# A new order of work for the last twenty steps of a recommendation kernel on Trainium2

## The chip, the cores and the metric

The kernel runs on one core of one Trainium2 chip. The core has a matmul engine (TensorE, PE in the profile, with its weight loads shown as PEld), three engines for elementwise work (VectorE or DVE, ScalarE or ACT, GpSimd or POOL) and SyncE (SP), which only issues DMAs. Each engine works through its own instructions in the order in which the program gives them, and they meet through semaphores. The metric is device time in microseconds; the median of several runs is compared.

## What is computed

The reference embeds a batch of 16384 users with 69 feature ids each, and one label id per user, from a table of 100001 rows of 96 floats. A small attention net weighs each feature's row against the label's row; the weighted rows are summed by 10 groups of features; a top net of three layers gives one number per user. In short:

```python
u  = emb[batch_user]                       # [B, 69, 96]
ql = emb[batch_label[:, 0]]                # [B, 96]
z  = concat([q, u, q - u, q * u])          # q: ql beside each feature
h  = dice(z @ W1 + b1, a1)                 # 64 wide
att = (h @ W2 + b2) @ W3 + b3              # one weight per feature
pre = where(batch_user < ITEM_NUM, u * att, 0)
pooled = einsum('gf,bfe->bge', window, pre)
x  = concat([pooled, ql])                  # 11 x 96
h  = dice(bn(x @ Wf1 + bf1), af1)          # 200 wide
h  = dice(bn(h @ Wf2 + bf2), af2)          # 80 wide
y  = h @ Wf3 + bf3
```

`dice(x)` is `(alpha * (1 - p) + p) * x` with `p` a sigmoid of the scaled `x`. All is float32.

## The kernel before

**Tiles.** The batch is cut into 32 blocks of 512 users (`BLK`). Of the 69 features 64 are "main" and 5 are "tail". A chunk is 512 rows of the table, four gathers of 128: a main chunk holds 8 users with their 64 features, a tail chunk holds one feature of all 512 users. A block has 64 + 5 = 69 chunks, and two chunks make a pair, so that there are 1104 pairs (`NPAIR`). The program is a list of steps, one per pair, and one more at the end. In the last block the tail chunks are put after the first 20 main ones (`chunk_of`).

**What a step holds.** `fetch(i)` (line 359) gathers the eight tiles of pair `i` by GpSimd's indirect DMA (line 266), transposes each on TensorE into a bank of PSUM (`ptr`), and lets VectorE copy the bank out twice: as it is (`uT`, line 376) and multiplied by the label's row (`quT`, line 379). For some chunks one of the four tiles comes instead by 128 row DMAs, each of one row, issued by SP or ACT (line 301) into a ring of buffers; `scalar_rows(i)` issues 20 of ACT's in each of the first 1088 steps.

`hidden(i)` (line 389) is called the sums in the change's description: four matmuls into one bank (`ph`, lines 396 to 403), two activations on ScalarE (lines 405, 406) and a product on VectorE (line 407) give `y`. `attend_tail` (line 419) turns `y` into weighted tail features. `attend_rows(b, n)` (line 409) takes `n` pairs from `b` on, a band: it forms rows of attention weights on TensorE (`prow`) and copies them on ScalarE (`row`). `spread(b, n)` (line 427) transposes a band (`patt`) and lets VectorE form the pooling weights `rw` (line 436). `pool(i)` (line 448) multiplies the gathered tiles with these weights into the bank `acc`, of which there is one, and VectorE copies the sums into `pooled` (line 470).

**The top net.** `top_steps(n, cols)` (line 542) cuts it into ten works: four parts of the first layer for each half of its 200 outputs (`top1`, line 489, with `dice` on ScalarE and VectorE after the fourth), the second layer (`top2`) and the third (`top3`, or `top3_last` for the last users). The last block's users are taken in four quarters of 128 columns, and `quarter[r]` is the list of ten works of quarter `r`.

**The order of work.** No scheduler moves anything: `plan` maps a step to a list of works, `at(step, ...)` appends to it, and the loop at the end (line 681) calls them in that order. The order of the works is therefore the order on each engine's queue. With `c = NPAIR - CLOSE = 1096`, the steps before `c - 8` follow one pattern: rows of bands of four, tails three steps behind the gathers, sums two behind, poolings seven behind (`POOL_LAG`). From `c - 8` on the poolings, and from `c` on everything, are written out step by step; in steps `c + 3` to `c + 7` some works are called between the two chunks of a `fetch`.

**Buffers.** Gathered pairs live in 15 buffers (`upool`). PSUM has eight banks: two for transpositions (`ps_tr`), two for the sums (`ps_h`), two for rows, spreads and tails (`ps_x`), one for the poolings (`ps_acc`) and one for the top net (`ps_m`). The second half of the first layer takes a bank of `ps_h` instead of `ps_m` in the last two quarters.

Of the kernel before, what the change touches and what calls it, by code (L numbers as in the profile page):

```python
# [18 lines left out]
P = 128  # L19
B, F, E, G = 16384, 69, 96, 10  # L20
# [5 lines left out]
BLK = 512  # L26
NBLK = B // BLK
# [5 lines left out]
NQ = BLK // P  # L33
NT = NCH * 4
NCOL = NT + NQ
NPAIR = NBLK * NCH // 2
# [4 lines left out]
POOL_LAG = 7  # L41
# [3 lines left out]
EARLY = 20  # L45

CLOSE = 8


ROW_BYTES = 4 * E  # L50
# [65 lines left out]
def rec_kernel(  # L116
# [372 lines left out]
    def top1(n, cols, h, part, p1):  # L489

        if part == 0:

            banks, tag = (ps_h, "h") if n == NBLK - 1 and cols.start >= BLK // 2 and h == 1 else (ps_m, "m")
            p1 = banks.tile([DH, BLK], F32, tag=tag, name=f"p1_{n}_{h}_{cols.start}")[:, cols]
        for k in range(part * KTOP // 4, (part + 1) * KTOP // 4):
            if k < NTAIL:
                w, x = V[:, k], pres[n][:, k, cols]
            elif k == NTAIL:
                w, x = wf1[:, G], qTs[n % 2][0:E, cols]
            else:  # L500
                w, x = wf1[:, k - NTAIL - 1], pooled[n][:, k - NTAIL - 1, cols]
            nc.tensor.matmul(p1, w[:, h * DH : (h + 1) * DH], x, start=(k == 0), stop=(k == KTOP - 1))  # L502
# [37 lines left out]
    pooled, pres, x1s, x2s, qs, us, hs, ys, bands, rws, p1s = ({} for _ in range(11))  # L540

    def top_steps(n, cols):


        def half(h, part):
            if n not in x1s:
                x1s[n] = xpool.tile([DH, 2, BLK], F32, tag="x1", name=f"x1_{n}")
            p1s[n] = top1(n, cols, h, part, p1s.get(n))

        steps = [lambda h=h, part=part: half(h, part) for h in range(2) for part in range(4)]  # L550
        steps.append(lambda: x2s.__setitem__(n, top2(n, cols)))
# [12 lines left out]
    def pool_of(k):  # L564
        return lambda: pool(k)

    def hidden_of(k):
        return lambda: ys.__setitem__(k, hidden(k, *hs[k]))

    def tails_of(k):  # L570
        def work():
            uT = hs.pop(k)[0]
            for j in range(2):
                if chunk_of(2 * k + j)[1] >= NMAIN:
                    attend_tail(k, j, ys[k], uT)

        return work

    def fetch_of(k, between=()):
        def work():  # L580
            for j in range(2):
                n = chunk_of(2 * k + j)[0]
                if n not in pooled:
                    pooled[n] = bpool.tile([E, G, BLK], F32, tag="pooled", name=f"pooled{n}")
                    pres[n] = xpool.tile([E, NTAIL, BLK], F32, tag="pre", name=f"pre{n}")
            u, uT, quT = fetch(k, lambda: [w() for w in between])
            us[k], hs[k] = u, (uT, quT)

        return work
# [4 lines left out]
    def at(step, *work):  # L594
        plan.setdefault(step, []).extend(work)
# [14 lines left out]
    def scalar_rows(i):  # L610

        row, stop = i * ACT_ROWS, min((i + 1) * ACT_ROWS, len(ACT_CHUNKS) * P)
        while row < stop:
            s, start = divmod(row, P)
            n = min(P - start, stop - row)
            by_scalar.fetch(s, start, start + n)
            row += n

    c = NPAIR - CLOSE
    for i in range(c):  # L620
        if i >= 3 and (i - 3) % 4 == 3:
            at(i, rows_of(i - 6, 4))
        if i >= 3:
            at(i, tails_of(i - 3))
        if i >= 4 and (i - 4) % 4 == 3:
            at(i, spread_of(i - 7, 4))
        if i >= 2:
            at(i, hidden_of(i - 2))
        at(i, lambda i=i: scalar_rows(i))
        if i < c - CLOSE:  # L630
            if i >= POOL_LAG:
                at(i, pool_of(i - POOL_LAG))
        else:

            for k in {0: (-15, -14), 1: (-13,), 3: (-12, -11), 4: (-10, -9), 7: (-8, -7)}.get(i - c + 8, ()):
                at(i, pool_of(c + k))
        at(i, fetch_of(i))

    at(c, pool_of(c - 6), pool_of(c - 5), tails_of(c - 3), hidden_of(c - 2), fetch_of(c))
    at(c + 1, tails_of(c - 2), hidden_of(c - 1), fetch_of(c + 1))  # L640
    at(c + 2, rows_of(c - 4, 4), tails_of(c - 1), hidden_of(c), spread_of(c - 4, 4), pool_of(c - 4), fetch_of(c + 2))
    at(c + 3, pool_of(c - 3), pool_of(c - 2), hidden_of(c + 1), fetch_of(c + 3, [hidden_of(c + 2)]))
    at(c + 4, pool_of(c - 1), fetch_of(c + 4, [hidden_of(c + 3)]))
    at(c + 5, rows_of(c, 4), spread_of(c, 4), pool_of(c), fetch_of(c + 5, [hidden_of(c + 4)]))
    at(c + 6, pool_of(c + 1), pool_of(c + 2), fetch_of(c + 6, [hidden_of(c + 5)]))
    at(c + 7, pool_of(c + 3), rows_of(c + 4, 2), fetch_of(c + 7, [spread_of(c + 4, 2), hidden_of(c + 6)]))

    for n in range(NBLK):
        first, end = n * NCH // 2, ((n + 1) * NCH - 1) // 2
# [12 lines left out]
    for f in range(NTAIL):  # L662
        at(2 + 2 * f, lambda f=f: tail_weights(f))

    quarter = [top_steps(NBLK - 1, slice(r * P, (r + 1) * P)) for r in range(NQ)]
    for s, step in enumerate([1, 1, 1, 2, 2, 2, 2, 3, 3, 3]):
        at(c - 8 + step, quarter[0][s])
    for s, step in enumerate([5, 5, 5, 5, 6, 6, 6, 6, 7, 9]):
        at(c - 8 + step, quarter[1][s])

    d = NPAIR
# [82 lines left out]
```

## Time and profile before

| what | value |
|---|---|
| median of 3 runs | 16757.55 us (16755.94 to 16759.19) |
| the profiled execution's own time | 10782.2 us |
| its span, first to last instruction | 10780.4 us |
| PE busy | 8756.9 us in 41797 matmuls |
| DVE busy | 4235.1 us |
| ACT busy, without its DMA issues | 1884.4 us |
| POOL busy | 8110.8 us |
| gathers | 8463 of main and tail rows, 128 of label rows |
| row DMAs | 25472 by SP, 21760 by ACT |
| granted TensorE clock, mean | 0.749 of full speed |

The profile describes one execution. Its own time is far from the median of the other runs, and the profile does not say why; durations of single instructions come from this one execution. A group of instructions is named by its line, engine and operation and by the tiles it writes and reads, with its busy time, the mean duration of one, and the idle time of its engine just before it. "issue" stands for idle time in which the engine waited for nothing that the profile shows. A matmul of float32 data shows as two records.

### The profile page before, as it was taken

How to read it: one execution, taken by the hardware profiler on the slowest of the kernel's cores; microseconds unless marked ns; L12 is line 12 of the kernel's file. 1: busy time of each engine (PE TensorE's matmuls, PEld its weight loads, DVE VectorE, ACT ScalarE, POOL GpSimd, SP SyncE). 2: the span in 40 equal slices, each digit the busy share in tenths (PEclk: the TensorE clock that was granted, in tenths of full speed). 3: DMA queues.
4: the chain of work that ended last, by engine and by line, in shares of the span. 5: the costliest groups of instructions: out<-in, count | busy, mean ns of one | idle time of the engine just before them, and what ended most of it. 6: DMA issues, size and time to landing. Idle time of an engine off the chain costs nothing.

```text
span 10780.4 us, 204439 instructions
## 1 busy us (share of the span) xinstructions
PE 8756.9 (81%) x41797; PEld 4310.8 (40%) x41797; DVE 4235.1 (39%) x7535; ACT 1884.4 (17%) x2761; POOL 8110.8 (75%) x8597
## 2 busy tenths in 40 slices
PE   6888888888887788877888788888887887888888
PEld 3434444434433344433433344333343343443335
DVE  4333333333333333333333343333333334333333
ACT  1111111111111111111111111111111111111112
POOL 7777777777777777777777777777777777777776
PEclk7777777677777777777777777777777777777778
DMA  2222222222222222222222222222222222222221
GB/s 50 42 42 42 45 42 42 42 42 45 42 42 42 45 42 42 42 42 45 42 42 42 42 44 42 42 42 42 44 42 42 42 42 44 42 42 42 42 42 34
DMA packets 372495, 460.70 MB, mean 43 GB/s; under 512 B 232114, under 2 KB 232626, under 8 KB 371106
## 3 DMA queue, kind: packets, MB, share of 16 engines
q0 software_dynamic: 274912, 422.81, 18.9%
q1 hardware_dynamic: 52802, 16.36, 1.0%
q10 hardware_dynamic: 43520, 8.44, 0.7%
q14 instruction: 925, 7.58, 0.2%
q8 instruction: 336, 5.51, 0.2%
HBM read 446.81 MB, written 0.07 MB: 41 GB/s over the span
## 4 chain that ended last, share of the span: by engine, by line
POOL 40%; PE 21%; issue 19%; DMA 12%; ACTq 6%; ACT 2%; DVE 1%; POOLq 0%
POOL u L266 40%; DMA u<-in_rows,ids 12%; ACTq L301 4%; PE acc L325 4%; PE p L502 4%; PE ph L399 3%; PE ph L403 3%; PE ptr L325 2%; PE prow L414 1%; ACTq L286 1%; PE pa L423 1%; ACT y L405 1%; POOL q L266 1%; PE ph L396 1%; PE ph L401 1%
## 5 line engine op out<-in xcount | busy, mean ns | idle before, releaser
L266 POOL DMA_INDIRECT u<-in_rows,ids x8463 | 7989.1, 944 | 2583.5 <-issue 2389.6
L325 PE MATMUL ptr<-ident,u 128*96 128x128 f32 x8463 | 1925.1, 332 | 1606.1 <-DMA u<-in_rows,ids 1555.6
L407 DVE TENSOR_TENSOR y<-ph,y 128x512 f32<-128x512 f32 x1104 | 763.5, 692 | 4972.6 <-ACT y L406 4699.0
L325 PEld LDWEIGHTS acc<-rw,u 128*96 128x96 f32 x15702 | 1674.4, 188 | 1332.5 <-issue 840.4
L325 PEld LDWEIGHTS ptr<-ident,u 128*96 128x96 f32 x8463 | 1131.6, 151 | 2282.7 <-DMA u<-in_rows,ids 1853.2
L325 PE MATMUL acc<-rw,u 128*96 128x20 f32 x15702 | 1792.0, 259 | 212.0 <-DVE rw L436 177.6
L376 DVE COPY uT<-ptr 96x512 f32<-96x512 f32 x2208 | 1489.0, 674 | 739.9 <-PE ptr L325 737.5
L405 ACT ACTIVATE y<-ph 128x512 f32<-128x512 f32 x1104 | 658.8, 597 | 6119.1 <-PE ph L403 3304.1
L399 PE MATMUL ph<-uT,A 128*64 128x512 f32 x4096 | 1598.9, 856 | 0.0
L403 PE MATMUL ph<-quT,wn 96*64 96x512 f32 x4416 | 1540.5, 767 | 0.0
L379 DVE TENSOR_TENSOR quT<-ptr,qT 96x512 f32<-96x512 f32 x2048 | 1379.1, 673 | 0.0
L406 ACT ACTIVATE y<-y,wn,na1c 128x512 f32<-128x512 f32 x1104 | 897.9, 813 | 36.6
L403 PEld LDWEIGHTS ph<-quT,wn 96*64 96x64 f32 x4416 | 429.4, 183 | 1002.5 <-issue 1001.8
L502 PE MATMUL p<-pooled,wf 96*100 96x512 f32 (+1 forms) x1400 | 667.7, 624 | 0.0
L414 PE MATMUL prow<-y,v 128*32 128x512 f32 x2208 | 507.2, 885 | 65.4 <-DVE y L407 57.6
L399 PEld LDWEIGHTS ph<-uT,A 128*64 128x64 f32 x4096 | 259.6, 172 | 609.6 <-issue 605.5
L416 ACT COPY row<-prow 128x512 f32<-128x512 f32 (+1 forms) x277 | 161.6, 583 | 1733.2 <-issue 675.0
L470 DVE COPY pooled<-acc 96x160 f32<-96x160 f32 x1008 | 420.5, 417 | 99.1 <-PE acc L325 97.6
L502 PE MATMUL p<-pre,V 96*100 96x512 f32 (+1 forms) x700 | 398.0, 714 | 11.1 <-DVE x L485 10.8
L502 PEld LDWEIGHTS p<-pooled,wf 96*100 96x100 f32 x1400 | 249.6, 190 | 316.5 <-issue 316.5
L436 DVE SCALAR_TENSOR_TENSOR rw<-patt,bb,wn 128x320 f32<-128x320 f32 x554 | 276.1, 539 | 116.8 <-PE patt L431 114.7
L485 DVE SCALAR_TENSOR_TENSOR x<-p,wf,g 100x512 f32<-100x512 f32 (+3 forms) x105 | 73.9, 704 | 523.6 <-ACT g L484 523.5
(72 smaller groups left out, 2706.1 us busy)
## 6 DMA issues: line engine op xcount, KB each, us to landing
ring<-in_rows SPq DMA_DIRECT2D x25472, 0.4 KB
ring<-in_rows ACTq DMA_DIRECT2D x21760, 0.4 KB
u<-in_rows,ids POOLq DMA_INDIRECT x8463
ids<-in_idx SPq DMA_DIRECT2D x8, 560.0 KB, 3.9
q<-in_emb,ids POOLq DMA_INDIRECT x128
wf<-in_far SPq DMA_DIRECT2D x1, 1209.0 KB, 8.3
wn<-in_near SPq DMA_DIRECT2D x1, 236.0 KB, 3.4
offsets<-in_single_rows SPq DMA_DIRECT2D x1, 192.0 KB, 2.5
```

What stands on the lines that cost most here:

```text
L266: nc.gpsimd.indirect_dma_start(out=dst, out_offset=None, in_=table, in_offset=bass.IndirectOffsetOnAxis(ap=index, axis=0),)
L301: d = self.engine.dma_start(out=ring[r : r + 1, b], in_=row_bytes[:, bass.ds(self.values[r], ROW_BYTES)]).then_inc(self.sems[k], 16)
L325: ins = op(out, ring[:, at[0]].bitcast(F32) if at else u[:, 4 * (c % 2) + t, :], other, **how)
L376: nc.vector.tensor_copy(uT[j][0:E], ptr)
L379: nc.vector.tensor_tensor(quT[:, j, :].rearrange("e (s f) -> e s f", f=FM), ptr.rearrange("e (s f) -> e s f", f=FM), by_field(q[:, k * NS ...
L399: nc.tensor.matmul(p, As[n % 2][:, k // 4, :], uT[j], start=True, stop=False)
L403: nc.tensor.matmul(p, Wp, quT[:, j, :], start=False, stop=True)
L405: nc.scalar.activation(y, ph, AF.Sigmoid, scale=S_DICE)
L406: nc.scalar.activation(y, y, AF.Identity, bias=a1c, scale=na1c)
L407: nc.vector.tensor_mul(y, ph, y)
L414: nc.tensor.matmul(pr[32 * k : 32 * (k + 1), :], v2, ys[b + k], start=True, stop=True)
L502: nc.tensor.matmul(p1, w[:, h * DH : (h + 1) * DH], x, start=(k == 0), stop=(k == KTOP - 1))
```

## The change

The plan of the last twenty steps, `c - 12` to `c + 7`, and of the work after them is written anew.

- The regular pattern ends at `c - 12`. From there on the sums run one step behind the gathers (`hidden_of(i - 1)`), the tails two behind, the rows and spreads come in bands of two pairs in every other step, and the poolings of two pairs, four and three behind, in the steps between. The first six steps are a passage from the old distances to the new ones.
- Nothing is called between the two chunks of a `fetch` any more.
- `QUARTERS` gives, for each of the first three quarters and each of their works, the step relative to `c` in which it is done. The first quarter moves from steps `c - 7` to `c - 5` to steps `c - 12` to `c - 7`, the second from `c - 3` to `c + 1` to `c - 5` to `c`. The third, which was done after the last gathers, moves to `c + 3` to `c + 7`, but for its last work.
- The last step's order is new too: the first parts of both halves of the last quarter are done ahead of the last poolings, and the store of all but the last 128 results ahead of them as well.
- Only the last quarter takes a bank of `ps_h` for its second half. `p1s` is kept per half, since parts of both halves may now be open together.

```diff
+QUARTERS = [
+    [-12, -12, -11, -11, -10, -10, -9, -9, -8, -7],
+    [-5, -5, -5, -4, -3, -3, -3, -2, -1, 0],
+    [3, 3, 3, 4, 5, 5, 5, 6, 7],
+]
...
-            banks, tag = (ps_h, "h") if n == NBLK - 1 and cols.start >= BLK // 2 and h == 1 else (ps_m, "m")
+            banks, tag = (ps_h, "h") if n == NBLK - 1 and cols.start == BLK - P and h == 1 else (ps_m, "m")
...
-            p1s[n] = top1(n, cols, h, part, p1s.get(n))
+            p1s[n, h] = top1(n, cols, h, part, p1s.get((n, h)))
...
-    for i in range(c):
+    for i in range(c - 12):
...
-        if i < c - CLOSE:
-            if i >= POOL_LAG:
-                at(i, pool_of(i - POOL_LAG))
-        else:
-
-            for k in {0: (-15, -14), 1: (-13,), 3: (-12, -11), 4: (-10, -9), 7: (-8, -7)}.get(i - c + 8, ()):
-                at(i, pool_of(c + k))
+        if i >= POOL_LAG:
+            at(i, pool_of(i - POOL_LAG))
         at(i, fetch_of(i))
 
-    at(c, pool_of(c - 6), pool_of(c - 5), tails_of(c - 3), hidden_of(c - 2), fetch_of(c))
-    at(c + 1, tails_of(c - 2), hidden_of(c - 1), fetch_of(c + 1))
-    at(c + 2, rows_of(c - 4, 4), tails_of(c - 1), hidden_of(c), spread_of(c - 4, 4), pool_of(c - 4), fetch_of(c + 2))
-    at(c + 3, pool_of(c - 3), pool_of(c - 2), hidden_of(c + 1), fetch_of(c + 3, [hidden_of(c + 2)]))
-    at(c + 4, pool_of(c - 1), fetch_of(c + 4, [hidden_of(c + 3)]))
-    at(c + 5, rows_of(c, 4), spread_of(c, 4), pool_of(c), fetch_of(c + 5, [hidden_of(c + 4)]))
-    at(c + 6, pool_of(c + 1), pool_of(c + 2), fetch_of(c + 6, [hidden_of(c + 5)]))
-    at(c + 7, pool_of(c + 3), rows_of(c + 4, 2), fetch_of(c + 7, [spread_of(c + 4, 2), hidden_of(c + 6)]))
+    for i in range(c - 12, NPAIR):
+        band = i - 3 if (i - c) % 2 and i > c - 11 else None
+        if i == c - 12:
+            at(i, pool_of(c - 19), tails_of(c - 15), hidden_of(c - 14))
+        elif i == c - 11:
+            at(i, pool_of(c - 18), tails_of(c - 14), rows_of(c - 16, 4))
+        elif i == c - 10:
+            at(i, pool_of(c - 17), pool_of(c - 16), pool_of(c - 15))
+        elif i == c - 9:
+            at(i, pool_of(c - 14))
+        elif i == c - 8:
+            at(i, pool_of(c - 13), pool_of(c - 12))
+        elif i == c - 7:
+            at(i, pool_of(c - 11))
+        elif band is None:
+            at(i, pool_of(i - 4), pool_of(i - 3))
+        if band is not None:
+            at(i, rows_of(band, 2))
+        if i > c - 12:
+            at(i, tails_of(i - 2))
+        at(i, hidden_of(i - 1), lambda i=i: scalar_rows(i))
+        if i == c - 11:
+            at(i, spread_of(c - 16, 4))
+        if band is not None:
+            at(i, spread_of(band, 2))
+        for r, steps in enumerate(QUARTERS):
+            at(i, *[work for step, work in zip(steps, quarter[r]) if c + step == i])
+        at(i, fetch_of(i))
...
-    for s, step in enumerate([1, 1, 1, 2, 2, 2, 2, 3, 3, 3]):
-        at(c - 8 + step, quarter[0][s])
-    for s, step in enumerate([5, 5, 5, 5, 6, 6, 6, 6, 7, 9]):
-        at(c - 8 + step, quarter[1][s])
...
-    at(d, pool_of(c + 4), hidden_of(c + 7), pool_of(c + 5), *quarter[2][0:4], rows_of(c + 6, 2), quarter[2][4])
-    at(d, spread_of(c + 6, 2), *quarter[2][5:8], pool_of(c + 6), quarter[2][8], pool_of(c + 7))
-    at(d, quarter[2][9], quarter[3][0], lambda: store(B // P - 1), *quarter[3][1:])
+    d, last = NPAIR, quarter[3]
+    at(d, pool_of(c + 4), hidden_of(c + 7), pool_of(c + 5), quarter[2][9], last[0], rows_of(c + 6, 2))
+    at(d, last[4], lambda: store(B // P - 1), spread_of(c + 6, 2), pool_of(c + 6), pool_of(c + 7))
+    at(d, *last[1:4], *last[5:])
```

More of the change, by code (lines that the diff above doesn't have):

```diff
@@ new lines, in rec_kernel @@
+        at(i, fetch_of(i))
+    quarter = [top_steps(NBLK - 1, slice(r * P, (r + 1) * P)) for r in range(NQ)]
+    for i in range(c - 12, NPAIR):
[26 more added lines that the diff above has]
+        at(i, fetch_of(i))
@@ L663, in rec_kernel @@
         at(2 + 2 * f, lambda f=f: tail_weights(f))
-    quarter = [top_steps(NBLK - 1, slice(r * P, (r + 1) * P)) for r in range(NQ)]
-    for s, step in enumerate([1, 1, 1, 2, 2, 2, 2, 3, 3, 3]):
-        at(c - 8 + step, quarter[0][s])
-    for s, step in enumerate([5, 5, 5, 5, 6, 6, 6, 6, 7, 9]):
-        at(c - 8 + step, quarter[1][s])
-    d = NPAIR
-    at(d, pool_of(c + 4), hidden_of(c + 7), pool_of(c + 5), *quarter[2][0:4], rows_of(c + 6, 2), quarter[2][4])
-    at(d, spread_of(c + 6, 2), *quarter[2][5:8], pool_of(c + 6), quarter[2][8], pool_of(c + 7))
-    at(d, quarter[2][9], quarter[3][0], lambda: store(B // P - 1), *quarter[3][1:])
+    d, last = NPAIR, quarter[3]
+    at(d, pool_of(c + 4), hidden_of(c + 7), pool_of(c + 5), quarter[2][9], last[0], rows_of(c + 6, 2))
+    at(d, last[4], lambda: store(B // P - 1), spread_of(c + 6, 2), pool_of(c + 6), pool_of(c + 7))
+    at(d, *last[1:4], *last[5:])
     with tc.manual_schedule():
```

## The prediction

> **What bounds the kernel now.** I read the page first, then who waited for whom on POOL, then stretches of the span side by side, then the timeline of the last 300 us. The page gives the span and the largest groups:
>
> ```profile
> span 10780.4 us, 204439 instructions
> PE 8756.9 (81%) x41797; PEld 4310.8 (40%) x41797; DVE 4235.1 (39%) x7535; ACT 1884.4 (17%) x2761; POOL 8110.8 (75%) x8597
> ...
> L266 POOL DMA_INDIRECT u<-in_rows,ids x8463 | 7989.1, 944 | 2583.5 <-issue 2389.6
> L325 PE MATMUL ptr<-ident,u 128*96 128x128 f32 x8463 | 1925.1, 332 | 1606.1 <-DMA u<-in_rows,ids 1555.6
> ```
>
> POOL is "only" 75% busy, yet its idle time is 0.30 us ahead of each gather and is called issue. The waits of POOL say that nothing else ever holds it:
>
> ```profile
> POOL u L266 <- issue: 2389.6, 7828, 0.3
> POOL u L266 <- DMA u<-in_rows,ids: 79.4, 260, 0.3
> POOL u L266 <- PE ptr L325: 78.8, 258, 0.3
> ```
>
> No wait is longer than 0.3 us, so POOL never stops for a buffer: 8591 gathers x (0.944 + 0.304) us = 10722 us of the 10780. A full step of eight gathers takes 10.0 us. What the kernel can win at its end is the time after the last gather, and whatever PE has left undone by then. The stretches and the timeline show that end:
>
> ```profile
> 10480.00:10570.00 90.00, 77.57 (x342) 37.13 (x343) 30.75 (x56) 15.33 (x22) 68.05 (x73) 0.84 0.19 41
> 10570.00:10736.00 166.00, 138.76 (x810) 89.77 (x810) 71.65 (x131) 34.78 (x55) 125.33 (x133) 0.79 0.19 40
> 10736.00:10781.00 45.00, 38.81 (x277) 28.59 (x275) 13.29 (x30) 10.54 (x20) 0.00 (x0) 0.88 0.01 4
> ```
>
> ```profile
> 10734.61 0.95 POOL L266 DMA_INDIRECT u<-in_rows,ids  x1 [0.30 <-issue]
> ...
> 10745.98 0.64 PE L325 MATMUL ptr<-ident,u 128*96 128x128 f32 x4
> ...
> 10752.18 1.32 PE L502 MATMUL p<-pre,V 96*100 96x128 f32 x10
> ...
> 10778.18 0.24 SPq L538 DMA_DIRECT2D out<-r  x1
> ```
>
> The columns of the stretches are the time, then PE, PEld, DVE, ACT and POOL busy, then granted clock. The last gather ends at 10735.56, the span 44.8 us later, and PE is busy for 38.8 of the last 45 us. PE is also late: if the k-th gather in the trace is paired with the k-th transposition, the lag is 4 to 6 us at the median through the run and 1.5 us at least. From 10490 us (the top net of block 30, then quarters of block 31) it is 15 to 33 us, and still 10.8 us at the last one. So this profile has a PE backlog over all 20 steps that change.
>
> [...] 0.73 granted in 10200 to 10480, 0.84, 0.79 and 0.88 in the three stretches above. [...] the trace's least lag of 1.5 us from the end of the gather instruction [...] is what I use. [...] here the profiled execution took 10782.2 us and the median of the runs shown is 16757.55[...]. Nothing in this profile says which resource is slower there: 5975 us over 8591 gathers is 0.70 us more for each.
>
> **The change part by part.** POOL's and SP's instruction orders are the same before and after; no gather and no row DMA moves there. ACT keeps its 20 row DMAs ahead of each of steps c-12 to c-9, with the activations of the sums around them. Nothing ahead of step c-12 (c = 1096) differs on any engine. So the effect must lie in the last 20 steps, 200 us of this profile.
>
> 1. *Third quarter ahead of the last gathers.* Nine of its ten parts leave the end. In the timeline they are 1.32 + 0.38 + 2.35 us (first half), 1.12 + 0.46 + 0.38 + 2.35 (second half) and 0.68 (second layer): 9.0 us as rows, 7.9 without their overlaps of 0.1 to 0.2. The tenth (0.36 us and a DVE operation of 0.18) stays. Its last inputs are the poolings of step c+2, and it starts at c+3, so it waits for no data. Its second half now uses the single bank of ps_m, but a step of 10 us later, when the first half's 1.3 us of ACT and DVE are over: nothing.
>
> 2. *The end, added anew from the start of the last transposition* (durations from the end of this profile). Transposition and the two copies 0.27 + 0.69 + 0.68 and gaps, 1.9 us, with pooling c+4 (1.46) beside them. Sums 2.0, to 3.9. ACT 0.60 + 0.81 and DVE 0.69, to 6.1, with pooling c+5 (1.5) and the third layer (0.36) beside them. DVE's copy and result 0.42 + 0.18, to 6.8; this frees the bank. Part 0 of the last quarter 1.1, rows 1.05, part 4 1.1, transposition of the results 0.27, to 10.4, which covers ACT's 0.58 copy of the rows. Spread 0.46 and DVE's weights 0.68, to 11.6. Pooling c+6, copy, pooling c+7, copy (1.46, 0.6, 1.53, 0.6), to 15.8. Rest of the last quarter 2.35 + 2.8, to 21.0. Two activations with their small matmuls and the DVE operations after them (1.4, 0.45, 1.35, 0.58, 0.34), to 25.2. The store issue and what lies after it, 2.2 as in this profile: 27.4. The trace of before has 10780.4 - 10746.35 = 34.05 for the same. **The end is 6.65 us shorter.** What covered the quarter's 7.9 us before is partly waiting that now shows (for DVE's weights and copies), which is why not all 7.9 come back.
>
> 3. *What the same 7.9 us cost ahead of the end.* If PE has slack there, nothing: a step of 10 us has about 8.4 us of matmul (138.8 us in 166). If PE is behind, as in this profile, they come back one for one. Lost with them: the waits that the new order opens up. In the timeline of before from 10570 to 10746, PE waits 3.0 us for the first quarter's second half, 1.4 and 1.4 for its next layers, 2.1 for DVE's weights, and 0.7, 0.7, 0.65 for the band of step c+5: 9.9 us, all where a step's result is wanted at once. The waits for ACT behind its row DMAs (4.5 and 4.4) stay.
>
> 4. *Sums one step behind, rows by pairs, poolings by pairs.* Four bands of four become eight of two: 4 x (2 x 0.46 - 0.66) = 1.0 us more PE, 4 x (2 x 0.66 - 1.01) = 1.2 us more DVE, 4 x 0.58 = 2.3 us more ACT after its row DMAs have ended; DVE and ACT are idle for half of it. Two poolings in one step wait for the single accumulator bank; before has 6.4 us of this in six places (0.5 to 1.9), seven places now make about 8.4, so +2. New: the sums follow their own step's transpositions. DVE needs 4 x 0.68 us for the copies; in the steps with rows PE has only some 1 us of other work first, so up to 1.5 us shows. It is not in the trace of before: 0 if PE is waiting for gathers anyway, 12 us over eight steps if not. I take 6 for a PE that is behind.
>
> Sum for a PE with slack: -6.65. For a PE behind as in this profile: -6.65 + 7.9 - 9.9 + 1.0 + 2 + 6 = +0.35, thus 10782.6 against 10782.2, with ends of -12 (no new waits and a denser, faster clock) and +7 (all of the 12 us).
>
> **Which of the two the runs shown are in.** They take 15.2 us a step instead of 9.8. If gathers or row DMAs are what is slower, PE has about 15.2 - 9.6 = 5.6 us of slack in each step and the backlog cannot last: -6.65. If PE or everything is slower, the backlog stays and the second sum holds, times 16757.55/10782.2 = 1.554: +0.5 with ends of -19 and +11. Three runs within 3.3 us look like a fixed pace rather than a throttled PE, so I take the first. **Forecast: 16757.55 - 6.65 = 16751 us.**
>
> **Rivals.**
> A. *PE behind in the timed runs too, nothing gained.* For: the backlog above. Against: the slack that 15.2 us a step would give. Time 16758 us.
> B. *Waits opened and backlog gone.* The rows and quarters now stand a step apart from their results; if PE drains all of its excess (10.8 - 1.5 = 9.3 us) as well as the shorter end, -6.65 - 9.3 = -16, to -25 when scaled. For: 9.9 us of waits removed. Against: 7.9 us of matmul moved in. Time 16737 us.
> C. *Slower: sums wait for their own step's copies.* The matmuls of the sums (L399 before) stand first in PE's order, so the transpositions of the next gathers queue behind them, then DVE, then the next sums. At 1.5 us in each of 20 steps it is 30 us, less the 6.65 and 9.9: +13, or 16771 us and, scaled, 16778. It decides once the shown wait is over 0.83 us a step ((6.65 + 9.9) / 20) with PE behind. Against: half the steps have 3 us of poolings ahead of the sums.
> D. *The change does nothing visible*, because ACT's row DMAs or the last result chain set the end anyway: within 3 us of before. The chain recounted above speaks against it.
>
> **How the numbers follow.** Forecast 0.45, A and D together 0.27, B 0.15, C 0.13. The range reaches from a little under B to C's near side: 16734 to 16768. Faster or slower by over 0.2% (33.5 us, about what a measurement of this kernel can tell from no change) would need most of the 44.8 us after the last gather to go, or 1.7 us of uncovered wait in every one of 20 steps on top of losing the gain. I give 0.05 to each side's far ends together with what I have not thought of: 0.05 faster, 0.91 same, 0.04 slower.
>
> **What the profile after would show.** Right: the last gather ends near 10735.6 as before, with POOL still waiting for no buffer; the third quarter's 64 matmuls stand ahead of the last transposition; from there to the end about 27 us instead of 34. Step 3 and 4 show in the lag of the last transposition: near 2 us speaks for B, 10 to 16 for the sum with a backlog, over 20 for C, and then PE's waits name DVE's copies ahead of L399's successor. Wrong: POOL waiting for PE, a wait over 1 us for the bank of ps_m, or a change in the part ahead of 10540 us.

## The result, and the profile after

The changed kernel takes 16770.82 us at the median of 19 runs, the kernel before 16756.62 us beside it; the ratio is 1.0007 with a 95% interval of 0.9999 to 1.0015. No difference is shown: the interval reaches from 2 us faster to 25 us slower. The forecast was 16751 us with a range of 16734 to 16768; the median lies 3 us above that range.

One fact has to come first, because it decides which traces may be laid side by side. The same kernel runs at two paces, and each chip showed one of them in all of its runs. (No chip is on record at two times, so whether the pace belongs to the chip or to the time stays open.) The kernel before took 16525 to 16780 us at the median on three chips (here chips 13, 3 and 5) and 10780.76 us on a fourth (chip 12). The profile on which the prediction rests is of the second kind, the runs shown with it are of the first, and so is the profile of the changed kernel. The page of the changed kernel, its span, engines and the chain that ended last by engine and by line:

```profile
span 16723.9 us, 204484 instructions
...
PE 8962.0 (54%) x41813; PEld 4588.0 (27%) x41813; DVE 4202.2 (25%) x7543; ACT 1884.9 (11%) x2765; POOL 8121.3 (49%) x8597
...
SPq 61%; issue 36%; PE 1%; ACTq 0%; DVE 0%; DMA 0%; another core or an unknown queue 0%; ACT 0%; POOL 0%; DVEq 0%
SPq L306 53%; SPq L291 8%; ACTq L306 0%; PE p L507 0%; PE ph L404 0%; PE acc L330 0%; DMA ring<-in_rows 0%; PE ph L408 0%; PE ptr L330 0%; PE patt L436 0%; PE prow L419 0%; DVE uT L381 0%; ACTq L291 0%; DVE quT L384 0%
```

```profile
L271 POOL DMA_INDIRECT u<-in_rows,ids x8463 | 7999.2, 945 | 8424.1 <-PE ptr L330 2844.9
...
L330 PE MATMUL ptr<-ident,ring 128*96 128x128 f32 x369 | 138.4, 375 | 4123.9 <-DMA ring<-in_rows 4037.6
```

The waits of POOL, which never exceeded 0.3 us in the profile before:

```profile
POOL u L271 <- PE ptr L330: 2844.9, 309, 63.0
POOL u L271 <- issue: 2232.5, 7317, 0.3
POOL u L271 <- PE acc L330: 1955.7, 152, 35.7
```

A gather still takes 0.945 us. But the chain runs along SP's row DMAs (line 306, line 301 before), PE waits 4037.6 us for the tiles that they fill, and POOL waits for up to 63 us for PE, which has to free its 15 buffers. At this pace the row DMAs set the time of the bulk, and the gathers do not. The timeline of SP shows the slower pace of these DMAs: 14 of them in 10.10 us here, 10 in 3.20 us where the kernel before runs at the other pace (experiment e8):

```profile
8251.83 10.10 SPq L306 DMA_DIRECT2D ring<-in_rows  x14
```

```profile
5000.79 3.20 SPq L301 DMA_DIRECT2D ring<-in_rows  x10
```

Over the whole trace SP's row DMAs start 0.652 us apart in the mean at this pace, 0.406 at the other. The median is 0.322 us at both: not every one is slower, but at this pace many distances are some 0.7, 1.4 or 2.1 us instead. The same holds for the unchanged kernel on such a chip (e1 below).

The end looks different from what the prediction took for it. The last gather ends at 16586.7 us and SP's last row starts at 16602.7, 121 us before the end. From there PE has only its own backlog. The stretches from SP's last row to the first transposition of step c, from there to the last transposition, and to the end (columns: time, then PE, PEld, DVE, ACT and POOL busy, then granted clock):

```profile
16602.70:16627.00 24.30, 21.75 (x106) 12.08 (x106) 8.53 (x17) 5.27 (x10) 0.00 (x0) 0.71 0.00 1
16627.00:16690.40 63.40, 58.26 (x316) 34.09 (x317) 26.59 (x51) 14.87 (x25) 0.00 (x0) 0.80 0.00 1
16690.40:16723.90 33.50, 25.64 (x156) 18.94 (x154) 8.52 (x21) 5.28 (x11) 0.00 (x0) 0.75 0.01 3
```

The last stretch, forecast at 27.4 us, takes 33.5, with 156 matmul records instead of 224 but at a clock of 0.75 instead of 0.89. Its timeline, with the groups that grew:

```profile
16694.68 1.06 PE L404 MATMUL ph<-uT,A 128*64 128x512 f32 x1
...
16694.88 2.41 PE L408 MATMUL ph<-quT,wn 96*64 96x512 f32 x3
...
16699.91 1.59 PE L507 MATMUL p<-pre,V 96*100 96x128 f32 x8 [0.95 <-DVE res L527]
16701.43 1.92 PE L419 MATMUL prow<-y,v 128*32 128x512 f32 x4
...
16707.67 2.75 PE L330 MATMUL acc<-rw,u 128*96 128x20 f32 x16 [0.52 <-DVE pooled L475]
...
16711.20 3.75 PE L507 MATMUL p<-pooled,wf 96*100 96x128 f32 x20
...
16721.63 0.24 SPq L543 DMA_DIRECT2D out<-r  x1
```

Set against the prediction's count from the last transposition (16690.43): sums done at 6.9 us instead of 3.9, results copied at 9.4 instead of 6.8, rows and parts 0 and 4 at 14.3 instead of 10.4, spread at 15.4 (11.6), poolings at 20.4 (15.8), last quarter's matmuls at 27.1 (21.0), the chain after them at 31.2 (25.2), end 33.5 (27.4). All of the 6 us is lost inside matmul groups: +3.0 in the sums, +1.3 in rows and parts, +0.8 in the poolings, +1.5 in the last quarter. The stages of ACT and DVE came out as counted.

### The profile page after: what moved, and what is told of

Same layout as the page of the kernel before. It is cut to its first block, busy times and chain, and to the rows that moved or that the text cites. A ratio compares the mean times of both kernels' runs of the same rounds, so it can differ in the third digit from the quotient of the medians.

```text
span 16723.9 us, 204484 instructions
## 1 busy us (share of the span) xinstructions
PE 8962.0 (54%) x41813; PEld 4588.0 (27%) x41813; DVE 4202.2 (25%) x7543; ACT 1884.9 (11%) x2765; POOL 8121.3 (49%) x8597
## 4 chain that ended last, share of the span: by engine, by line
SPq 61%; issue 36%; PE 1%; ACTq 0%; DVE 0%; DMA 0%; another core or an unknown queue 0%; ACT 0%; POOL 0%; DVEq 0%
SPq L306 53%; SPq L291 8%; ACTq L306 0%; PE p L507 0%; PE ph L404 0%; PE acc L330 0%; DMA ring<-in_rows 0%; PE ph L408 0%; PE ptr L330 0%; PE patt L436 0%; PE prow L419 0%; DVE uT L381 0%; ACTq L291 0%; DVE quT L384 0%
## 5 line engine op out<-in xcount | busy, mean ns | idle before, releaser
L271 POOL DMA_INDIRECT u<-in_rows,ids x8463 | 7999.2, 945 | 8424.1 <-PE ptr L330 2844.9
L330 PE MATMUL acc<-rw,u 128*96 128x20 f32 x15702 | 1914.4, 267 | 1154.0 <-issue 409.2
L330 PEld LDWEIGHTS acc<-rw,u 128*96 128x96 f32 x15702 | 1794.2, 199 | 2265.9 <-issue 1211.4
L330 PE MATMUL ptr<-ident,ring 128*96 128x128 f32 x369 | 138.4, 375 | 4123.9 <-DMA ring<-in_rows 4037.6
L330 PE MATMUL ptr<-ident,u 128*96 128x128 f32 x8463 | 1520.2, 330 | 388.2 <-issue 306.0
L404 PE MATMUL ph<-uT,A 128*64 128x512 f32 x4096 | 1633.1, 850 | 56.8 <-issue 42.2
L330 PEld LDWEIGHTS ptr<-ident,u 128*96 128x96 f32 x8463 | 1191.0, 161 | 527.0 <-issue 459.2
L330 PEld LDWEIGHTS ptr<-ident,ring 128*96 128x96 f32 x369 | 56.9, 154 | 4185.5 <-issue 3747.1
L419 PE MATMUL prow<-y,v 128*32 128x512 f32 x2208 | 700.2, 851 | 901.6 <-issue 448.8
L507 PE MATMUL p<-pooled,wf 96*100 96x512 f32 (+1 forms) x1400 | 722.5, 657 | 57.3 <-issue 55.5
L419 PEld LDWEIGHTS prow<-y,v 128*32 128x32 f32 x2208 | 82.2, 127 | 1231.2 <-issue 691.6
```

What stands on the lines that cost most here:

```text
L271: nc.gpsimd.indirect_dma_start(out=dst, out_offset=None, in_=table, in_offset=bass.IndirectOffsetOnAxis(ap=index, axis=0),)
L330: ins = op(out, ring[:, at[0]].bitcast(F32) if at else u[:, 4 * (c % 2) + t, :], other, **how)
L404: nc.tensor.matmul(p, As[n % 2][:, k // 4, :], uT[j], start=True, stop=False)
L419: nc.tensor.matmul(pr[32 * k : 32 * (k + 1), :], v2, ys[b + k], start=True, stop=True)
```

## The experiments

In all of them "half clock" is time for which the trace records a granted clock of one half. The profile of before has 1078 records of the granted clock and that of the changed kernel 1346: each is of 1 or of 0.5, and all but the last of each trace are 3.413 us long or a multiple of it. "The tail" is the time from SP's last row to the end.

**e1, the kernel before on a chip of the slow pace** (no edit).

> The kernel before, unchanged, for a profile at the pace of the timed runs. Theory (row DMAs of SP and ACT set that pace): span 16.7 ms; SP's row DMAs start 0.65 us apart in the mean instead of the 0.41 of the first profile; PE waits some 4000 us for rows of the ring; POOL waits for PE some 5000 us; from SP's last row DMA to the end some 120 to 130 us, with no gather left to wait for, so that PE works off a backlog of eight or nine steps. Rival (gathers slower): a gather takes about 1.6 us of POOL instead of 0.944, POOL waits for nothing, PE has slack at the end.

Measured: 16744.83 us in a single run, span 16743.1. PE waits 4070.4 us for the rows' tiles and POOL 2928.9 us for PE's transpositions, so the picture is not the change's doing. SP's last row starts 122.3 us before the end. Its last three stretches, cut as above:

```profile
16620.80:16648.50 27.70, 24.09 (x154) 16.32 (x153) 10.80 (x21) 5.98 (x11) 7.55 (x8) 0.75 0.06 15
16648.50:16709.00 60.50, 53.41 (x292) 31.43 (x291) 29.50 (x53) 13.29 (x20) 0.00 (x0) 0.79 0.00 1
16709.00:16743.10 34.10, 28.53 (x224) 23.74 (x221) 7.55 (x19) 8.30 (x17) 0.00 (x0) 0.89 0.01 3
```

This is the trace to compare with. The tail is 122.3 us before and 121.2 after: the last stretch is 0.6 us shorter, and the one ahead of it, which took in the third quarter, 2.9 longer. PE has slack through the bulk (53% busy) and little in the tail (106 of 122 us busy), so work put ahead of the last transposition is not hidden there.

**e2 and e9, the third quarter alone.** The kernel before, with the third quarter's first nine works at c+4 to c+6 in place of the last step, and nothing else of the change:

```diff
-            banks, tag = (ps_h, "h") if n == NBLK - 1 and cols.start >= BLK // 2 and h == 1 else (ps_m, "m")
+            banks, tag = (ps_h, "h") if n == NBLK - 1 and cols.start == BLK - P and h == 1 else (ps_m, "m")
...
+    at(c + 4, *quarter[2][0:4])
+    at(c + 5, *quarter[2][4:8])
+    at(c + 6, quarter[2][8])
-    at(d, pool_of(c + 4), hidden_of(c + 7), pool_of(c + 5), *quarter[2][0:4], rows_of(c + 6, 2), quarter[2][4])
-    at(d, spread_of(c + 6, 2), *quarter[2][5:8], pool_of(c + 6), quarter[2][8], pool_of(c + 7))
+    at(d, pool_of(c + 4), hidden_of(c + 7), pool_of(c + 5), rows_of(c + 6, 2))
+    at(d, spread_of(c + 6, 2), pool_of(c + 6), pool_of(c + 7))
```

> The kernel before with one part of the change alone: the third quarter's first nine works moved to steps c+4 to c+6. Theory (PE works off a backlog from the last row to the end): moved work comes back one for one, from the last row DMA to the end the same as before within 3 us, time 0 to -3 us. Rival (PE has slack at the end, as forecast): -6 to -9 us.

> The kernel before with the third quarter alone moved, timed again. On the chip whose gathers set the pace (10.78 ms): theory (the loss of 20 us comes from the rewritten steps c-12 to c-1, not from this part) -4 to +2 us; rival (moving 7.9 us of matmul ahead of a PE that is late costs by itself) +6 us or more. On the chip whose row DMAs set the pace (16.76 ms): within the scatter, and 118 to 119 us from SP's last row to the end.

Measured: ratio 1.0000 (0.9991 to 1.0009) on chip 13 and 1.0008 (0.9999 to 1.0017) on chip 3; tail 118.6 and 120.0 us; last transposition to end 31.7 and 30.6 us, half of it or a third at half clock (14.4 and 10.4 us). In these profiles the tail is 2 to 4 us shorter, which is less than the tails of one kernel differ between profiles (e12), and the times show no gain; the interval of e9, 2 us faster at most, leaves out the 6.65 us that the forecast gave for the end.

**e3 and e4, no row DMAs.** All tiles but those of one chunk for each of SP and ACT come by gathers; what is computed stays the same. e3 has the kernel before, e4 the changed one.

```diff
-SP_CHUNKS = [2 * (int(5.5 * s) + 6) + 1 for s in range(199)]
+SP_CHUNKS = [2 * (int(5.5 * s) + 6) + 1 for s in range(1)]
-ACT_CHUNKS = [2 * ((s + 1) * P // ACT_ROWS + 2) for s in range(170)]
+ACT_CHUNKS = [2 * ((s + 1) * P // ACT_ROWS + 2) for s in range(1)]
```

> The order of before, with one chunk each of SP and ACT left as row DMAs and all the others gathered by POOL: 8830 or so gathers. Theory (row DMAs set the pace): 8959 x 1.248 + 55 = 11.2 ms. Rival (gathers set it, 1.94 us each): 17.4 ms.

> The same with the order of after. Against the run with the order of before: -6.65 us if PE has slack ahead of the last gathers (the step of the forecast in its own regime), 0 with ends of -12 and +7 if PE is behind there as in the first profile, +13 if the sums' waits for their own step's copies decide.

Measured: 13504.5 and 13488.99 us, ratios 0.806 (0.8046 to 0.8073) and 0.805 (0.8038 to 0.8062). So the row DMAs do set the pace on this chip. But the time stays well above 8958 gathers x 1.248 us = 11180 us; PE now shows idle stretches called issue of up to 51.9 us, in which nothing that the profile shows is waited for. Slow rows are a part of the slower pace and not all of it. The 15 us between e3 and e4 are within the scatter of four runs each, so they decide nothing about the order.

**e5 and e6, the end of the changed kernel.** e5 puts 44 extra matmuls, whose results nobody reads, into the gaps of the last step; e6 gives it e2's last step.

```diff
-    at(d, pool_of(c + 4), hidden_of(c + 7), pool_of(c + 5), quarter[2][9], last[0], rows_of(c + 6, 2))
+    at(d, pool_of(c + 4), warm(4), hidden_of(c + 7), pool_of(c + 5), warm(4), quarter[2][9], last[0], rows_of(c + 6, 2))
...
```

```diff
+    at(d, pool_of(c + 4), hidden_of(c + 7), pool_of(c + 5), rows_of(c + 6, 2))
+    at(d, spread_of(c + 6, 2), pool_of(c + 6), pool_of(c + 7))
+    at(d, quarter[2][9], last[0], lambda: store(B // P - 1), *last[1:])
```

> The kernel after, with 44 extra matmuls (each 128 rows by 96 columns by 128, written to a transposition bank and read by nobody) put into the last step where TensorE waits for ACT or DVE. Theory (after the last gathers the new order has so little matmul work that the granted clock drops to a half for 16.6 of the last 33.5 us, against some 7 us before, and this eats the gain of the shorter end): granted clock of the last 33 us at least 0.9 instead of 0.75, and from the last transposition to the end less than 31 us in spite of the extra work, which is some 44 x 0.11 = 5 us at full clock where nothing hides it. Rival (the wait chain itself was miscounted): clock higher or not, 34 to 39 us.

> The kernel after with the last step in the order of the run that moves the third quarter alone: sums, poolings, rows, spread, poolings, then the last quarter at one stretch. Theory (the new order of the last step, two parts of the last quarter put into gaps, is what differs between 33.4 and 31.7 us from the last transposition): 31.7 us, within 0.5. Rival (what the steps before leave behind, the clock above all): 33 us or more.

Measured on chip 12, in one run each: last transposition to end 33.3 us in e5 and 34.3 in e6, against 33.5 in the changed kernel there. In e5 the clock of that stretch rises from 0.76 to 0.95 and the time at half clock falls from 16.4 to 3.4 us, yet the filling costs what the clock gives. Both expected lengths, below 31 us and 31.7, were missed. The other order of the last step (e6) is worth nothing, and filling the end with useless work is no cure. That the low clock stretches the end is not shown by e5, but by profiles of one and the same last step (under step 2 below).

**e7 and e8, both kernels on the chip of the faster pace** (no edits).

> The kernel after, unchanged, timed again. Theory (nothing is gained or lost beyond 2 us; the 14 us of the first comparison are scatter of the row DMAs' pace): ratio within 0.0008 of 1, sign open; from SP's last row DMA to the end 121 us. Rival (the new order slows the row DMAs): again 10 to 15 us slower.

> The kernel before, unchanged, timed against itself, as a measure of the scatter: median within 10 us of its twin, ratio 1 with an interval of about 0.0008 either way; if it differs by 10 us or more, the 14 us of the first comparison say nothing.

Measured: 10800.43 us for the changed kernel, ratio 1.0016 (1.0009 to 1.0022); 10779.88 for the kernel before, ratio 1.0000. Here the change costs 19.7 us. The stretches from c-12 to c-8 and their sums from c-16 to the end, of e8 and then of e7:

```profile
10567.10:10599.90 32.80, 22.41 (x118) 11.62 (x118) 12.76 (x24) 6.13 (x9) 24.88 (x27) 0.80 0.18 42
...
sum 254.90, PE 209.46 PEld 136.34 DVE 102.25 ACT 51.70 POOL 160.24; mean PE 41.89 PEld 27.27 DVE 20.45 ACT 10.34 POOL 32.05
```

```profile
10592.70:10641.70 49.00, 36.18 (x210) 25.40 (x209) 16.16 (x31) 7.67 (x14) 37.09 (x40) 0.77 0.17 41
...
sum 274.80, PE 229.28 PEld 142.42 DVE 103.49 ACT 53.41 POOL 160.04; mean PE 45.86 PEld 28.48 DVE 20.70 ACT 10.68 POOL 32.01
```

All of the 19.9 us is busy PE time (+19.8), with 16 more matmul records (of the bands' transpositions) among 1233; PE's idle time is the same, 45.4 and 45.5 us. Two things make it busy for longer.

- *The clock.* Half clock covers 106.3 us of e8's stretch and 125.6 of e7's. It also covers other matmuls: of the 200 records of the sums 100 instead of 64, of the 160 of the top net that read `pooled` 60 instead of 28, of the 80 that read `pre` 8 instead of 23. The wide matmuls take longer then (rows of two pairs 1.05 us at full clock and 1.92 at half), so 19.3 us more of half clock account for about half of the 19.8 us, by estimate.
- *The rows in bands of two.* On PE a band of two pairs takes as long as a band of four, as a band from the first profile of before and one from e7 show, both at full clock:

```profile
10617.25 1.07 PE L414 MATMUL prow<-y,v 128*32 128x512 f32 x8
```

```profile
10617.58 1.05 PE L419 MATMUL prow<-y,v 128*32 128x512 f32 x4
```

The same 56 records of rows keep PE busy for 18.2 us in e7 and 11.6 in e8. Four bands more at 1.05 us each make some 4 us of the difference, by estimate; the rest fits the clock.

What remains, some 6 us, no run here takes apart. The profile of e7 is that of its slowest run (10814.98 us); the 19.7 us are a difference of medians, and that the stretches of one profile each differ by as much is in part chance.

**e10, the pair of poolings parted.** The changed kernel; in the steps of two poolings one stays ahead of the sums, the other moves behind them and the quarters:

```diff
-            at(i, pool_of(i - 4), pool_of(i - 3))
+            at(i, pool_of(i - 4))
...
+        if band is None and i > c - 7:
+            at(i, pool_of(i - 3))
         at(i, fetch_of(i))
```

> The kernel after with the two poolings of a step parted: one ahead of the sums as now, the other after them, ahead of the gathers' transpositions. Theory (two poolings in a row, 32 matmuls of 20 columns with a wait between, lower the granted clock, and the sums behind them then run at half of it): from c-8 to the last transposition less than 50 us at half clock instead of 56.1, fewer than 35 of the wide matmuls of the sums there at half, and the end 4 to 8 us earlier than the order of after; the waits of TensorE for the pooled sums fall from 12.9 us to under 5. Rival (clock and order of the poolings do not matter): only the waits go, 0 to -4 us.

Measured on chip 3: 16753.21 us, ratio to the kernel before 0.9986 (0.9979 to 0.9993); tail 92.4 us; from the first transposition of c to the last 47.7 us with no half clock (the changed kernel: 63.5 us, 25.7 of them at half clock); the end behind it unchanged at 33.3 us.

**e11, the pair kept and the gap filled.** The changed kernel, with eight extra matmuls between the two poolings:

```diff
-            at(i, pool_of(i - 4), pool_of(i - 3))
+            at(i, pool_of(i - 4), warm(8), pool_of(i - 3))
```

> The kernel after with eight extra matmuls (128 rows by 96 columns by 128, read by nobody) between the two poolings of a step, where TensorE waits for the accumulator bank anyway. Theory (the clock): half-clock time from c-8 to the end falls from 72.5 us to under 55 and the end comes 3 to 7 us earlier, in spite of 7 x 0.9 us of extra work. Rival (extra work only): clock up or not, 0 to +6 us.

Measured: ratio 0.9995 (0.9986 to 1.0004). From c to the last transposition 58.0 us at a clock of 0.97, 3.4 us at half; the 48 records of filling seen there take 7.3 us. With the order of the changed kernel kept and the gap covered, the wide matmuls of the sums run at the durations of e10 (618 and 598 ns in the mean against 618 and 596):

```profile
16695.00:16753.00 58.00, 56.21 (x366) 36.13 (x365) 26.73 (x51) 15.11 (x25) 0.00 (x0) 0.97 0.00 1
```

So it is the clock, and not where the poolings stand, that made them long; what was won is again spent on the filling.

**e12, the first two bands' rows copied by VectorE**, so that they don't stand behind ScalarE's row DMAs:

```diff
-        nc.scalar.copy(row, pr)
+        if b in (NPAIR - CLOSE - 16, NPAIR - CLOSE - 12):
+            nc.vector.tensor_copy(row, pr)
+        else:
+            nc.scalar.copy(row, pr)
```

> The kernel after with the copies of the bands c-16 and c-12 made by VectorE instead of ScalarE, which still has its row DMAs to issue in those steps. Theory (rows and spread in one step put TensorE behind ScalarE's 20 row DMAs): the two waits of TensorE for the copied rows, 3.1 and 3.3 us, go, and the end comes 3 to 6 us earlier than the order of after. Rival (the same row DMAs hold the next sums' activations): the waits move to the sums or the pooled sums, 0 to -1 us.

Measured: ratio 1.0002 (0.9993 to 1.0011). The stretch c-12 to c-8 takes 65.1 us against 64.4 in the profile of the changed kernel. No gain of its own is shown; at the faster pace, where e7 has PE wait 6.4 us for such copies (0.7 us in e8), it was not run. Its tail of 109.0 us is shorter all the same, through stretches that the edit does not touch, such as a last one of 29.0 us at a clock of 0.90; by this and by the 121.2 and 124.7 us of the changed kernel (e14), a single profile's tail is good to no better than some 10 us.

**e13, e14 and e15, the parted order against the changed kernel on one chip.** e13 is e10 again, e14 the changed kernel again, e15 is e10 with e12's edit.

> The split order once more (the two poolings of a step parted: one ahead of the sums, one just ahead of the fetch). Theory (the pair of poolings in a row lowers the matmul clock, and the wide matmuls behind it pay): on a chip with the slow row DMAs 15 to 30 us below the kernel before, c to the last transposition 45 to 52 us at a clock over 0.95 with under 5 us at half clock, and at least 10 us below the changed kernel of the same call. On a chip with the faster pace: 5 to 20 us below the changed kernel, so from 15 us above the kernel before to level with it. Rival (the gain of the first look was the scatter of the row DMAs): within 8 us of the changed kernel on either chip, with the same time at half clock.

> The changed kernel beside the split one. Theory: c to the last transposition 62 to 65 us with 20 us or more at half clock; slower than the split order by 10 us or more. Against the kernel before: within 15 us on a chip with slow row DMAs, 15 to 22 us slower on one with the faster pace. Rival: within 8 us of the split one.

> The split order and, with it, the bands of rows of steps c-16 and c-12 copied out by VectorE, so that they do not stand behind ScalarE's 20 row DMAs. If ScalarE's queue is a second cost in steps c-12 to c-8, the end stands 3 to 8 us earlier than in the split order alone. If the matmul clock is the only one, within 3 us of it in the stretch from c-12 to the end, and level with it in time.

Measured on chip 5, where the kernel before takes 16525.17 us: e13 16506.65 us, ratio 0.9989 (0.9981 to 0.9997); e14 16520.77, ratio 1.0001 (0.9992 to 1.0011); e15 16498.02, ratio 0.9984 (0.9977 to 0.9990). The mean of e13 is 16 us below that of e14 (95%: 4 to 28, by drawing again from the runs), so the gain of e10 was not scatter. e15 is 26 us below e14 (13 to 38); its 10 us below e13 (interval from -20 to +1) are not shown. The tails are 124.7 us in e14, 104.7 in e13 and 93.4 in e15. The stretch from the first transposition of c to the last, e14 and then e13:

```profile
16391.70:16455.20 63.50, 58.32 (x317) 34.29 (x317) 26.63 (x51) 14.99 (x25) 0.00 (x0) 0.80 0.00 1
```

```profile
16429.90:16479.10 49.20, 48.04 (x319) 30.25 (x318) 26.56 (x52) 13.82 (x23) 0.00 (x0) 0.97 0.00 1
```

The groups of PE in it, e14 and then e13 (busy, mean ns, idle before and its cause):

```profile
L404 PE MATMUL ph<-uT,A 128*64 128x512 f32 x28 | 12.7, 862 | 0.1
...
L330 PE MATMUL acc<-rw,u 128*96 128x20 f32 x94 | 10.7, 261 | 5.0 <-DVE pooled L475 3.8 <-DVE rw L441 1.2
L330 PE MATMUL ptr<-ident,u 128*96 128x128 f32 x64 | 10.4, 316 | 0.0
L419 PE MATMUL prow<-y,v 128*32 128x512 f32 x16 | 7.2, 806 | 0.1
```

```profile
L404 PE MATMUL ph<-uT,A 128*64 128x512 f32 x28 | 12.8, 683 | 0.0
...
L330 PE MATMUL acc<-rw,u 128*96 128x20 f32 x97 | 9.1, 237 | 1.2 <-DVE rw L441 1.2
L330 PE MATMUL ptr<-ident,u 128*96 128x128 f32 x64 | 8.4, 274 | 0.0
L419 PE MATMUL prow<-y,v 128*32 128x512 f32 x16 | 4.2, 605 | 0.0
```

And the timeline of PE in one step of two poolings each, step c+4 of e14 and then c+6 of e13, where the second pooling stands behind the sums:

```profile
16419.89 1.46 PE L330 MATMUL acc<-rw,u 128*96 128x20 f32 x16
16422.52 1.53 PE L330 MATMUL acc<-rw,u 128*96 128x20 f32 x16 [1.18 <-DVE pooled L475]
16423.99 1.92 PE L404 MATMUL ph<-uT,A 128*64 128x512 f32 x4
16425.69 1.93 PE L408 MATMUL ph<-quT,wn 96*64 96x512 f32 x4
```

```profile
16467.12 1.46 PE L330 MATMUL acc<-rw,u 128*96 128x20 f32 x16
16468.51 1.39 PE L404 MATMUL ph<-uT,A 128*64 128x512 f32 x4
16469.42 1.34 PE L408 MATMUL ph<-quT,wn 96*64 96x512 f32 x4
```

Two poolings in a row leave a gap of 1.2 us and then cost the sums behind them a third of their speed: 1.92 + 1.93 us in place of 1.39 + 1.34. The stretch takes 63.5 us in e14 and 49.2 in e13; of these 14.3 us, 4.0 are PE's idle time and 10.3 are shorter matmuls. Half clock covers 25.5 us of it in e14, 3.4 in e13. The kernel before, whose plan also has steps of two poolings, spends 25.8 us of its own stretch at half clock (e1). So the change did not add half clock there, and only the parted order is nearly rid of it. Whether the poolings are the reason in the kernel before too, no run shows.

## Why the prediction was wrong

**What bounds the kernel now** read the profile rightly and applied it to the wrong runs. On the chip of that profile the gathers set the bulk and PE carries a backlog; on the chips of the runs shown the row DMAs do.

**Which of the two the runs shown are in** is the step that failed. It named row DMAs as a possible cause, which e1 and e3 bear out, and concluded "PE has slack" from 15.2 us a step. That mean hides the shape. PE waits for one row tile for 22 us in the mean (4037.6 us in 186 waits), then has a burst of gathered tiles, up to the 15 buffers, and after SP's last row it works off the last burst for 120 us, 106 of them busy, and moved work does not hide there. Slack in the mean is not slack at the end. The prediction's own sign of being wrong, POOL waiting for PE, is there (2844.9 us). (The 9.6 us of PE work in that step has no source; its own count elsewhere is 8.4.) So the sum for a PE with slack, -6.65 us, was the wrong one to take: tail 122.3 us before, 121.2 after, and no difference in time.

The other sum, for a PE behind, gave about nothing (+0.35 us), which is rival A's place and near what the slow pace shows. That is partly luck: it was worked out for the pace of the first profile, and there the change costs 19.7 us (e7), outside its ends of -12 and +7. The steps below say which of its terms failed.

**Step 1** was right: 68 records left the end (224 in e1, 156 after; it counted 64), and no wait for the bank of ps_m shows. **Step 2** was mis-sized: 33.5 us (e14 33.4, e7 33.5) against 27.4. The durations were taken from an end at a clock of 0.89, with 7.4 us at half clock; this one has 0.75 and 16.7 us. Three other profiles with the same last step, e12, e11 and e13, have other clocks:

```profile
16727.50:16756.50 29.00, 21.22 (x156) 16.47 (x154) 8.48 (x21) 5.23 (x11) 0.00 (x0) 0.90 0.01 3
```

```profile
16753.00:16783.30 30.30, 22.44 (x156) 17.91 (x153) 8.43 (x21) 5.18 (x11) 0.00 (x0) 0.84 0.01 3
```

```profile
16479.10:16513.60 34.50, 26.64 (x156) 20.90 (x153) 8.41 (x21) 5.17 (x11) 0.00 (x0) 0.71 0.01 3
```

With 5.8, 9.6 and 20.1 us at half clock the end takes 29.0, 30.3 and 34.5 us: its length follows the clock. (e15 and e10 lie between, 31.9 us with 13.1 and 33.3 with 15.3.) Since 5.8 us at half clock still give 29.0, some 2 us of the 6 are not the clock. Against e1 the gain at the end was 0.6 us instead of 6.65.

**Step 3** had the right rule, that moved work comes back one for one if PE is behind, but its 9.9 us of removed waits did not become less idle time. From c to the last transposition PE's idle time falls from 7.1 us (e1) to 5.1, of which new waits for the accumulator are 3.8. At the faster pace, from c-16 to the end, it is 45.4 us before and 45.5 after. Waits went there, and others came: 6.4 us for ScalarE's copies of the rows (0.7 in e8) and 3.0 for the copies of a step's own gathers (none in e8).

**Step 4** had three terms wrong. It priced the bands of two at 1.0 us of PE for their transpositions and put the row matmuls themselves at nothing, though they take some 4 us more (e7). It priced the poolings by pairs at +2 us of waiting; in e7 PE waits 13.4 us for the accumulator in nine places, against 9.1 in eight in e8 and 6.4 in six in the first profile. And it left out the clock behind a pair of poolings. In c to the last transposition that is worth 10.3 us (e14 against e13), in a stretch in which the kernel before has as much half clock (25.8 us in e1, 25.5 in e14); over the whole of the changed steps e7 has 19.3 us more at half clock than e8. Its largest term, up to 12 us of sums waiting for their own copies, came in part: none in c to c+7, 3.0 us in one place ahead of them in e7, and 13.2 us in four places in the changed kernel at the slow pace, where PE also waits for rows.

**The rivals.** A is nearest on the slow chips. B fell: the tail did not shrink. D's number, within 3 us of before, is not excluded there (interval -2 to +25 us; e14 0.9992 to 1.0011), but its reason fell, since PE is busy for 106 of the last 121 us. C had the sign right on the faster chip, +19.7 where +13 was worked out, and the lag of the last transposition is over 20 us there (29.7 in e7, 7.7 in e8). But its mechanism fell: the 19.8 us are busy time, and only 3.0 us of waiting for DVE's copies show.

**The range** had no case in which the matmuls themselves take longer, and its upper side was C's waiting alone. The median is 3 us above it, which is less than the interval of the measurement; it is the step above that failed, and not these 3 us. The end of -12 in the second sum counted on a faster clock in a denser order. That was my estimate, and I never asked where the new order is thinner. The runs show the clock rise where gaps are filled: from 0.76 to 0.95 in the last stretch (e5), and from 0.80 in the changed kernel to 0.97 from c to the last transposition (e11).

**What stays open.** Why SP and PE stand still on the chips of the slower pace: between SP's row DMAs (0.652 us apart in the mean, 0.406 at the other pace) stand gaps of up to 2 us and more in which nothing that the profile shows is waited for, and without them PE has idle stretches of the same kind, up to 51.9 us (e3). No run here shows the cause. Also open: whether the parted order gains on the faster chip, where it was not run, and what of a pair of poolings lowers the clock. In e11 two runs of narrow matmuls follow each other as in the changed kernel, with the wait between them filled, and the clock stays up (0.97); so the narrowness alone does not do it, but no run has a wait between wide ones.

## What to carry to other kernels

Check that the profile and the timed runs have the same time before using one for the other, and read slack where the work lands, not as a mean. Before a group of matmuls is split, look in the trace whether its members ran side by side: here half a band of rows takes as long as a whole one (1.05 us against 1.07). Ask of a new order on TensorE what the wide matmuls stand behind: here two runs of narrow ones with a wait between them went with half clock behind them (25.5 us of it in e14, 3.4 in e13), and the longer matmuls cost more (10.3 us) than the waits (4.0 us). Parting the two poolings made a version that is faster than the kernel before (0.9986 and 0.9989, and 0.9984 with two bands copied by VectorE) and than the changed one (16 us, e13 against e14), at the slow pace; more than 0.2% it is not.

## What was not expected of the hardware

The pace of one and the same program differs between chips by up to 56%: 16525 to 16780 us on three, 10781 us on another. The gather's duration does not (944 to 946 ns), and on the slower pace PE stands still at times even with the row DMAs gone (up to 51.9 us, e3). There the time scatters by some 20 us to either side from run to run (16733.52 to 16779.90 us in 19 runs of the kernel before), more than the change itself moves it.

In the three profiles of the changed order on chip 12 (e5, e6, e7) a gather takes 945.6 ns in the mean instead of 943.9 (e8), from the start of the trace on, where the two programs are still alike; that is 14 us by the last gather. The order is not the reason, since e2 and e3, with the order of before or nearly so, have 946 ns. The reason is not known. The median of e7, 10800 us, lies 15 us below the time of its profiled run, 10815.
